# Weight sums formed with the first group's first unit, kept unsplit; more warm-up matmuls; the first gate blocks in another order

## The chip, the cores and the metric

The kernel runs on one core of one Trainium2 chip, as one program. The metric is device time in microseconds (us) of that program. Of the kernel before, three timed runs are given. Where a time stands at a place ("near 252 us"), it is counted from the start of the profiled span.

## The reference

The input is 2 x 1024 rows of 1024 numbers, in fp32. The first block of the network is a gated layer with a sparse gate; the second is a gated feed-forward layer with tiled weights and low-rank terms. Each ends in a residual sum and a layer norm. The change touches only the first half of the first block:

```python
s = silu(einsum('bsh,ih->bsi', x, w_gate))        # 2048 x 2752
_, idx = top_k(-abs(s), k)                        # k = 2752 // 2, per row
s = s with the entries at idx set to 0
s = s * einsum('bsh,ih->bsi', x, w_up)
return einsum('bsi,hi->bsh', s, w_down)
```

The largest half of each row of the gate, by magnitude, is kept exactly, so the gate product must be accurate. The kernel therefore splits each fp32 operand into a high and a low part and multiplies high by high, high by low and low by high.

## The kernel before

The 2048 rows are 16 tiles of 128 rows, in four groups of four tiles (`GT`). The first stage, `gate_up`, runs over groups g, within each over four units u of 688 of the 2752 columns, and within each unit first over the gate ("g") and then over the up product ("u"). It takes about 948 of the 1992 us. Then come the down product and the feed-forward layer, which the change doesn't edit.

A unit's weights are four blocks, B11, B12, B21 and B22: the first digit is the half of the contraction, the second the half of the unit's columns. Each is 128 x 1376 fp32, 688 KB. The up product takes the four blocks one by one, two products each. A product is here 24 matmuls into one pair of PSUM banks, 3.8 us. The gate of most units is done with seven products in place of eight, in Strassen's manner (`GATE`, L42), from blocks and from four weight sums T1 to T4 (`T_AT`, L44: T1 = B12 - B11, T2 = B22 - T1, T3 = B22 - B12, T4 = B21 - T2). Only the first gate of all (g = 0, u = 0) is done with the four plain blocks, in the order of `UP`.

One step is one block or sum. Its work is in three functions:

- `w_load` (L211) issues its DMA from SP, five steps ahead (`LOADS`), into a ring of three raw slots, `wr`.
- `w_prep` (L233), three steps ahead (`AHEAD`), splits it: ACT casts the high part into a ring `wh` (L165), and POOL subtracts it from the raw block into `wl` (L166). For the very first block DVE does the subtraction.
- `products` (L307) issues the matmuls: per product, 16 with the high part of the weights and then 8 with the low part.

`form` (L207) says how a step of the seven-product gate gets its sums. At 2, all four blocks are loaded at once, DVE forms the sums into tiles of the top-k pool (L250), they are split as above, and the split halves are stored to DRAM, two stores of 688 KB for each sum. At 1, in later groups, both halves are read back straight into `wh` and `wl`, with nothing for ACT or POOL to do. The sums are formed in group 0 for the units 1 to 3, and in group 1 for unit 0, which has no seven-product gate in group 0.

The x operands are split the same way, by ACT and DVE (`x_slot`, L191, with sums S1 to S4 formed by DVE at L196 to L201). Those of group 0 are made in the steps of the first unit.

What follows a product: in a plain gate, ACT applies Silu from PSUM (`gate`, L350); in a seven-product gate, `post` combines on DVE and ACT; in the up product, DVE multiplies by the gate result into `mt` (`up`, L358, the row L362). This reading frees the PSUM pair. There are four pairs; one of them stays with the warm-up tile, so that products rotate over three.

`topk` (L369) finds each row's threshold for the group before: six passes in which ACT (L403) counts three of the row tiles and DVE (L400) one, small DVE operations that narrow the bounds (L406 to L426), then two passes a tile (L430, L431) and a final one (L444). It takes its tiles from the same pool as the sums, tags a0 to a3. A scheduler sets the order of instructions on each engine from their dependences and estimated times, so that DVE's operations of `topk`, of `x_slot` and of the products lie mixed.

Ahead of the first stage, a loop (L110) issues `WARM` fp32 matmuls of 128 x 128, each two instructions, on an identity matrix. Their result isn't used.

Of the kernel before, what the change touches and what calls it, by code (L numbers as in the profile page):

```python
# [7 lines left out]
F = mybir.dt.float32  # L8
# [5 lines left out]
ALU = mybir.AluOpType  # L14
# [4 lines left out]
P = 128  # L19
# [9 lines left out]
CW = KH * BW  # L29
# [4 lines left out]
NPR = GT // 2  # L34
# [5 lines left out]
TKAT = (2, "g", 2)  # L40
CACHED = ("T1", "T2", "T3", "T4")
GATE = (("A11", "B11"), ("S2", "T2"), ("S3", "T3"), ("S1", "T1"), ("A12", "B21"), ("S4", "B22"), ("A22", "T4"))  # L42
UP = ("B11", "B21", "B12", "B22")
T_AT = ([("T1", "B12", "B11")], [("T2", "B22", "T1")], [("T3", "B22", "B12")], [], [], [], [("T4", "B21", "T2")])  # L44
LOV = ()
WARM = 14
TAILC = ((0, 512), (512, 768), (768, 1024))


# [13 lines left out]
class Kern:  # L63
# [7 lines left out]
    def run(self):  # L71
# [3 lines left out]
        with ExitStack() as es:  # L75
# [33 lines left out]
            warm = self.tpb()  # L109
            for i in range(WARM):  # L110
                nc.tensor.matmul(warm[:, i % 4, :], self.ident, self.ident, start=True, stop=True)
# [94 lines left out]

    def form(self, i):  # L207
        g, u, w, k = self.steps[i]
        return 0 if w == "u" or g + u == 0 else 2 if g == int(u == 0) else 1

    def w_load(self, i):  # L211
        nc = self.nc
        g, u, w, k = self.steps[i]
        f = self.form(i)
        b = GATE[k][1] if f else UP[k]
        W = self.A["wg" if w == "g" else "wu"]

        def load(q):
            r = self.wr.get()
            k0, n0 = (int(q[1]) - 1) * KH, int(q[2]) - 1  # L220
            self.lastd = nc.sync.dma_start(r.rearrange("p (a b) -> p a b", a=KH), W[2 * u + n0][:, k0 : k0 + KH, :])
            return r

        if f == 2:
            if k == 0:
                self.wb = {q: load(q) for q in ("B11", "B12", "B22", "B21")}
            self.wraw.append(self.wb)
        elif f and b in CACHED:
            self.wraw.append(None)
        else:  # L230
            self.wraw.append(load(b))

    def w_prep(self, i):  # L233
        nc, V = self.nc, self.nc.vector
        g, u, w, k = self.steps[i]
        f = self.form(i)
        b = GATE[k][1] if f else UP[k]
        raw = self.wraw.pop(0)
        hl = self.wh.get(), self.wl.get()
        self.wq.append(hl)  # L240
        if raw is None:
            for x, d in zip(hl, self.tw_d[u, b]):
                nc.sync.dma_start(x.bitcast(F), d)
            return
        if f == 2:
            if k == 0:
                tt = [self.tk.tile([P, 2, CW], F, tag=t, name="tw") for t in (("a3", "a2") if u == 0 else ("a0", "a1"))]
                self.tt = {f"T{j + 1}": tt[j // 2][:, j % 2] for j in range(4)}
            for o, x, y in T_AT[k]:
                V.tensor_tensor(self.tt[o], raw[x], raw.get(y, self.tt.get(y)), ALU.subtract)  # L250
            raw = raw.get(b, self.tt.get(b))
        self.split(*hl, raw, V if i == 0 else nc.gpsimd)
        if f == 2 and b in CACHED:
            for x, d in zip(hl, self.tw_d[u, b]):
                nc.sync.dma_start(d, x.bitcast(F))

    def gate_up(self):
        nc, V = self.nc, self.nc.vector
        ng = self.nt // GT
        self.steps = [(g, u, w, k) for g in range(ng) for u in range(NU) for w in "gu" for k in range(7 if w == "g" and g + u else 4)]  # L260
        self.xfull, self.tkg, self.xs, self.xraw, self.wraw, self.wq, self.li, self.wi = {}, None, {}, {}, [], [], 0, 0
        cc = {}
        xg = self.x_raw(0)
        next(xg)
        for i, (g, u, w, k) in enumerate(self.steps):
            while self.li < min(i + LOADS + 1, len(self.steps)):
                self.w_load(self.li)
                if self.li == 0:
                    list(xg)
                self.li += 1  # L270
            while self.wi < min(i + AHEAD + 1, len(self.steps)):
                j = self.steps[self.wi]
                if j[:2] == (0, 0):
                    for op in {("g", 0): ("A11", "A21"), ("g", 1): ("A12", "A22"), ("u", 1): ("S2",), ("u", 2): ("S1", "S3"), ("u", 3): ("S4",)}.get(j[2:], ()):
                        self.x_slot(op)
                self.w_prep(self.wi)
                self.wi += 1
            wh, wl = (x.rearrange("p (a b) -> p a b", a=KH) for x in self.wq.pop(0))
            if self.form(i):
                a = GATE[k][0]  # L280
                ps = self.pair()[:, :, :BW]
                self.products([(ps[:, p], self.xs[p, a]) for p in range(NPR)], wh, wl, True, True)
                self.post((g, u), k, ps, cc)
            else:
                h = k % 2
                if h == 0:
                    ps = [self.pair()[:, :, :BW] for j in range(2)]
                for j in range(2):
                    self.products([(ps[j][:, p], self.xs[p, f"A{j + 1}{h + 1}"]) for p in range(NPR)], wh, wl, h == 0, h == 1)
                if h:  # L290
                    (self.up if w == "u" else self.gate)((g, u), k // 2, ps, cc)
            if (u, w) == (NU - 1, "u") and g + 1 < ng:
                for op in (("S2", "S1", "S3", "S4"), (), ("A11", "A21"), ("A12", "A22"))[k]:
                    if op == "S2":
                        list(self.x_raw(g + 1))
                    with self.behind():
                        self.x_slot(op)
            if g and (u, w, k) == TKAT:
                self.tkg = self.topk(g - 1)
            if self.tkg:  # L300
                next(self.tkg, None)
            if (g, u, w, k) == (ng - 1, NU - 1, "u", 1):
                self.et = [self.tk.tile([P, NI], d, tag=f"a{j}", name=n) for j, (n, d) in enumerate((("em", F), ("eh", R), ("el", R)))]
                self.d0 = self.down(0, early=3)
                next(self.d0)
# [42 lines left out]
            )  # L348

    def gate(self, un, b, ps, cc):  # L350
        if b == 0:
            cc[un] = [self.ev.tile([P, NPR, 2, BW], F, tag=f"cc{t}", bufs=2, name=f"cc{t}") for t in range(2)]
        for t in range(2):
            self.nc.scalar.activation(cc[un][t][:, :, b], ps[t], AF.Silu)
            if b:
                self.put(self.sp_d, un, t, cc[un][t])

    def up(self, un, b, ps, cc):  # L358
# [585 lines left out]
```

## Time and profile before

| | us |
|---|---|
| median of 3 timed runs | 1996.35 |
| lowest and highest of them | 1995.55, 1996.76 |
| profiled execution, its own time | 1994.28 |
| its span in the profile | 1992.5 |

The busy time of the engines in each stage, and the DMA share there:

| stretch, us | PE | DVE | ACT | POOL | DMA share |
|---|---|---|---|---|---|
| group 0, 0 to 237 | 232.4 | 94.7 | 90.3 | 137.4 | 0.68 |
| group 1, 237 to 474 | 227.6 | 144.7 | 120.4 | 108.6 | 0.76 |
| group 2, 474 to 711 | 233.8 | 137.6 | 117.0 | 93.2 | 0.77 |
| group 3, 711 to 948 | 235.2 | 125.4 | 117.3 | 98.4 | 0.73 |
| down, 948 to 1500 | 519.0 | 336.0 | 234.2 | 354.1 | 0.56 |
| feed-forward, 1500 to 1992.5 | 452.9 | 378.6 | 287.2 | 230.6 | 0.62 |

The stretches are cut by hand where the stages change; neighbours overlap a little at a cut. PE is TensorE's matmuls; DVE, ACT and POOL are VectorE, ScalarE and GpSimd; SP is the engine whose queue issues the DMAs. A row of a timeline gives start, duration, engine, line, operation, output and inputs, shape, count and, in brackets, how long the engine stood idle before it and what it then waited for. The clock is the one that the throttle granted to TensorE, as a share of full speed.

### The profile page before, as it was taken

How to read it: one execution, taken by the hardware profiler on the slowest of the kernel's cores; microseconds unless marked ns; L12 is line 12 of the kernel's file. 1: busy time of each engine (PE TensorE's matmuls, PEld its weight loads, DVE VectorE, ACT ScalarE, POOL GpSimd, SP SyncE). 2: the span in 40 equal slices, each digit the busy share in tenths (PEclk: the TensorE clock that was granted, in tenths of full speed). 3: DMA queues.
4: the chain of work that ended last, by engine and by line, in shares of the span. 5: the costliest groups of instructions: out<-in, count | busy, mean ns of one | idle time of the engine just before them, and what ended most of it. 6: DMA issues, size and time to landing. Idle time of an engine off the chain costs nothing. (4 is left out here: it accounts for less than half of the span.)

```text
span 1992.5 us, 29245 instructions
## 1 busy us (share of the span) xinstructions
PE 1900.8 (95%) x10757; PEld 1762.0 (88%) x10757; DVE 1216.9 (61%) x1791; ACT 966.5 (49%) x1538; POOL 1022.3 (51%) x634
## 2 busy tenths in 40 slices
PE   9999999999999999999898899999998889999998
PEld 8999999999999999999777777777778779898897
DVE  5232646935477345852378935445587988879565
ACT  5323467315852358423575224334334756757363
POOL 5655463434344333344567666665684744626162
PEclk9999999999999999999999999999999999999999
DMA  6677696688757887676844555656556678575661
GB/s 236 240 255 262 216 338 217 237 332 300 271 204 243 338 296 246 249 260 249 293 141 124 182 185 170 208 170 186 169 161 220 227 266 315 176 275 178 221 214 64
DMA packets 156556, 455.14 MB, mean 228 GB/s; under 512 B 23700, under 2 KB 44308, under 8 KB 156408
## 3 DMA queue, kind: packets, MB, share of 16 engines
q1 hardware_dynamic: 156264, 452.97, 65.6%
q8 instruction: 85, 1.39, 0.3%
q14 instruction: 63, 0.52, 0.1%
q10 hardware_dynamic: 144, 0.26, 0.0%
HBM read 346.56 MB, written 106.56 MB: 227 GB/s over the span
## 5 line engine op out<-in xcount | busy, mean ns | idle before, releaser
L166 POOL TENSOR_TENSOR wl<-wr,wh 128x1376 fp32r<-128x1376 f32 (+2 forms) x205 | 598.1, 2925 | 464.3 <-ACT wh L165 441.2
L312 PE MATMUL mm<-wh,xh 128*128 128x344 f32 x1928 | 613.3, 322 | 16.7 <-ACT wh L165 7.1
L312 PE MATMUL mm<-wh,xl 128*128 128x344 f32 x1928 | 611.5, 321 | 0.0
L165 ACT CAST wh<-wr 128x1376 fp32r<-128x1376 f32 (+2 forms) x210 | 246.5, 1182 | 327.5 <-PE mm L312 194.4
L312 PEld LDWEIGHTS mm<-wh,xh 128*128 128x128 f32 x1928 | 364.8, 189 | 19.6 <-ACT wh L165 7.6
L312 PEld LDWEIGHTS mm<-wh,xl 128*128 128x128 f32 x1928 | 364.4, 189 | 0.0
L312 PE MATMUL mm<-wl,xh 128*128 128x344 f32 x1928 | 345.2, 321 | 0.0
L312 PEld LDWEIGHTS mm<-wl,xh 128*128 128x128 f32 x1928 | 313.1, 188 | 0.0
L642 PE MATMUL mm<-wl,mh 128*128 128x512 f32 x680 | 217.4, 400 | 14.5 <-POOL wl L166 14.5
L642 PE MATMUL mm<-wh,mh 128*128 128x512 f32 x680 | 219.4, 405 | 9.0 <-DVE acc L645 6.2
L403 ACT ACTIVATE jk<-a,cur 128x2752 int8<-128x2752 f32 x72 | 186.3, 2588 | 57.3 <-DVE cur L426 42.7
L642 PE MATMUL mm<-wh,ml 128*128 128x512 f32 x648 | 206.3, 398 | 0.0
L601 POOL TENSOR_TENSOR m<-m,ub 128x512 f32<-128x512 f32 (+2 forms) x93 | 108.4, 1165 | 156.8 <-DMA m<-m_d 100.2
L846 POOL TENSOR_TENSOR hf<-hf,gt 128x344 f32<-128x344 f32 x96 | 138.5, 1453 | 80.9 <-DVE gt L840 75.7
L833 PE MATMUL mm<-wh,fh 128*128 128x344 f32 x512 | 168.7, 330 | 11.7 <-DVE gt L840 8.0
L642 PEld LDWEIGHTS mm<-wl,mh 128*128 128x128 f32 x680 | 128.2, 191 | 46.0 <-POOL wl L166 18.6
L835 PE MATMUL mm<-wh,fl 128*128 128x344 f32 x512 | 165.8, 324 | 0.0
L834 PE MATMUL mm<-wl,fh 128*128 128x344 f32 x512 | 165.7, 324 | 0.0
L642 PEld LDWEIGHTS mm<-wh,mh 128*128 128x128 f32 x680 | 124.9, 191 | 34.9 <-issue 6.6
L645 DVE TENSOR_TENSOR acc<-acc,mm 128x1024 f32<-128x1024 f32 x96 | 116.4, 1213 | 52.2 <-PE mm L642 52.0
L600 ACT CAST ub<-u 128x512 bf16<-128x512 uint8 (+2 forms) x93 | 53.1, 571 | 193.4 <-POOL m L601 177.8
L642 PEld LDWEIGHTS mm<-wh,ml 128*128 128x128 f32 x648 | 122.6, 190 | 27.0
(185 smaller groups left out, 2856.6 us busy)
## 6 DMA issues: line engine op xcount, KB each, us to landing
wr<-wu SPq DMA_DIRECT2D x64, 688.0 KB
wr<-wd SPq DMA_DIRECT2D x84, 512.0 KB
wr<-wg SPq DMA_DIRECT2D x53, 688.0 KB
s_d<-cc SPq DMA_DIRECT2D x64, 344.0 KB
m_d<-mt SPq DMA_DIRECT2D x64, 344.0 KB
a<-s_d SPq DMA_DIRECT2D x64, 344.0 KB
wh<-wc_w SPq DMA_DIRECT2D x48, 344.0 KB
wl<-wc_w SPq DMA_DIRECT2D x48, 344.0 KB
```

Source lines behind the costliest of these rows:

```text
L165: self.nc.scalar.copy(hi, raw)
L166: (eng or self.nc.gpsimd).tensor_tensor(lo, raw, hi.bitcast(F), ALU.subtract)
L312: self.nc.tensor.matmul(o, l, r, start=start and n < m and n % (2 * KH) == 0, stop=stop and n >= m and (n - m) % KH == KH - 1)
L403: nc.scalar.activation(jk.bitcast(I8), av[j], AF.Sign, bias=t, scale=-1.0, accum_out=s)
L600: nc.scalar.copy(ub[:, :w], u[:, :w])
L601: nc.gpsimd.tensor_tensor(m[:, :w], m[:, :w], ub[:, :w], ALU.mult)
L642: nc.tensor.matmul(ps[:, h], a, b[:, h * 512 : (h + 1) * 512], start=i == 0, stop=i == len(ops) - 1)
L645: nc.vector.tensor_tensor(out, out, ps.rearrange("p a b -> p (a b)"), ALU.add)
L833: nc.tensor.matmul(o, fh[:, c, :], wh[:, c, :], start=c == 0, stop=False)
L834: nc.tensor.matmul(o, fh[:, c, :], wl[:, c, :], start=False, stop=False)
L835: nc.tensor.matmul(o, fl[:, c, :], wh[:, c, :], start=False, stop=False)
L846: G.tensor_tensor(hf[:, hs], hf[:, hs], gt, ALU.add)
```

## The change

It has three parts, all in the first stage.

- **Sums.** `form` gives 2 only in group 0. For unit 0, DVE forms the four sums while the plain gate of group 0 is prepared: T1 in its second step, T2 and T3 in its third, T4 in its fourth, in tiles a0 and a1. They are stored unsplit, four DMAs of 688 KB, at the preparation of the up product's last step. In the groups 1 to 3, unit 0 loads each sum through the raw ring and splits it on ACT and POOL like a block. The other units keep their stored halves; all sums now use the tiles a0 and a1.
- **Order.** The first gate takes its blocks in the order B11, B12, B22, B21 (`G0`), so that both pairs of column halves are open at once: the first two steps start them, the last two complete them, the second column half first. `gate` allocates its result with the second half and stores it with the first.
- **Warm-up.** `WARM` goes from 14 to 48, that is from 28 to 96 instructions.

```diff
+G0 = ("B11", "B12", "B22", "B21")
 UP = ("B11", "B21", "B12", "B22")
-WARM = 14
+WARM = 48
...
-        return 0 if w == "u" or g + u == 0 else 2 if g == int(u == 0) else 1
+        return 0 if w == "u" or g + u == 0 else 2 if g == 0 else 1
...
-        b = GATE[k][1] if f else UP[k]
+        b = GATE[k][1] if f else (G0 if w == "g" else UP)[k]
...
             if k == 0:
-                self.wb = {q: load(q) for q in ("B11", "B12", "B22", "B21")}
+                self.wb = {q: load(q) for q in G0}
             self.wraw.append(self.wb)
+        elif f and u == 0 and b in CACHED:
+            r = self.wr.get()
+            self.lastd = nc.sync.dma_start(r, self.tw_d[u, b][0])
+            self.wraw.append(r)
         elif f and b in CACHED:
...
+        if g + u == 0 and w == "g":
+            self.b0[b] = raw
         if f == 2:
             if k == 0:
-                tt = [self.tk.tile([P, 2, CW], F, tag=t, name="tw") for t in (("a3", "a2") if u == 0 else ("a0", "a1"))]
+                tt = [self.tk.tile([P, 2, CW], F, tag=t, name="tw") for t in ("a0", "a1")]
...
         self.split(*hl, raw, V if i == 0 else nc.gpsimd)
+        if g + u == 0 and w == "g" and k:
+            if k == 1:
+                tt = [self.tk.tile([P, 2, CW], F, tag=t, name="tw") for t in ("a0", "a1")]
+                self.tt = {f"T{j + 1}": tt[j // 2][:, j % 2] for j in range(4)}
+            for o, x, y in ((), T_AT[0], T_AT[1] + T_AT[2], T_AT[6])[k]:
+                V.tensor_tensor(self.tt[o], self.b0[x], self.b0.get(y, self.tt.get(y)), ALU.subtract)
+        if (g, u, w, k) == (0, 0, "u", 3):
+            for o in CACHED:
+                nc.sync.dma_start(self.tw_d[0, o][0], self.tt[o])
...
-                h = k % 2
-                if h == 0:
+                first = w == "g"
+                h = int((G0 if first else UP)[k][1]) - 1
+                n = int((G0 if first else UP)[k][2]) - 1
+                st, sp = (k < 2, k > 1) if first else (h == 0, h == 1)
+                if st:
                     ps = [self.pair()[:, :, :BW] for j in range(2)]
+                    pss[n] = ps
+                ps = pss[n]
                 for j in range(2):
-                    self.products([(ps[j][:, p], self.xs[p, f"A{j + 1}{h + 1}"]) for p in range(NPR)], wh, wl, h == 0, h == 1)
-                if h:
-                    (self.up if w == "u" else self.gate)((g, u), k // 2, ps, cc)
+                    self.products([(ps[j][:, p], self.xs[p, f"A{j + 1}{h + 1}"]) for p in range(NPR)], wh, wl, st, sp)
+                if sp:
+                    (self.up if w == "u" else self.gate)((g, u), n, ps, cc)
...
     def gate(self, un, b, ps, cc):
-        if b == 0:
+        if b:
             cc[un] = [self.ev.tile([P, NPR, 2, BW], F, tag=f"cc{t}", bufs=2, name=f"cc{t}") for t in range(2)]
         for t in range(2):
             self.nc.scalar.activation(cc[un][t][:, :, b], ps[t], AF.Silu)
-            if b:
+            if b == 0:
                 self.put(self.sp_d, un, t, cc[un][t])
```

In the built program, TensorE's order of the first gate is both products of B11, then one each of B12, B22 and B21 for one half of the rows (the first tile of each pair), then those of B12, B22 and B21 for the other half. B12's second product waits until ACT's first Silu has read a PSUM pair.

More of the change, by code (lines that the diff above doesn't have):

```diff
@@ L236, in w_prep @@
         f = self.form(i)
-        b = GATE[k][1] if f else UP[k]
+        b = GATE[k][1] if f else (G0 if w == "g" else UP)[k]
         raw = self.wraw.pop(0)
@@ L261, in gate_up @@
         self.xfull, self.tkg, self.xs, self.xraw, self.wraw, self.wq, self.li, self.wi = {}, None, {}, {}, [], [], 0, 0
-        cc = {}
+        cc, self.b0 = {}, {}
+        pss = {}
         xg = self.x_raw(0)
```

## The prediction

> **What bounds the kernel now.** I read the page's first part, then the waits in front of TensorE, then the stretches where the change acts, engine by engine.
>
> ```profile
> PE 1900.8 (95%) x10757; PEld 1762.0 (88%) x10757; DVE 1216.9 (61%) x1791; ACT 966.5 (49%) x1538; POOL 1022.3 (51%) x634
> ```
>
> TensorE is busy 95% of 1992.5 us and every other engine about half. So an edit is worth what it does to TensorE's gaps, plus the slow matmuls that follow a gap. The change touches three places in the gate and up stage. The first is the start (PE, timeline):
>
> ```profile
> 1.43 6.24 PE L111 MATMUL mm<-ident 128*128 128x128 f32 x28 [1.43 <-POOL ident masks.py:199]
> 10.55 0.42 PE L312 MATMUL mm<-wh,xh 128*128 128x344 f32 x1 [2.88 <-ACT wh L165]
> ...
> 31.62 0.42 PE L312 MATMUL mm<-wh,xh 128*128 128x344 f32 x1 [0.33 <-ACT cc L354]
> ```
>
> [...]28 warm-up instructions run to 7.67, TensorE idles 2.88, the first product starts at 10.55. The granted clock, by microsecond (PEclk is the third figure from the right):
>
> ```profile
> 10.00:11.00 1.00, 0.45 (x2) 0.46 (x3) 0.47 (x1) 1.00 (x3) 0.00 (x0) 0.92 1.10 440
> 11.00:12.00 1.00, 1.00 (x5) 1.00 (x5) 1.00 (x1) 1.00 (x4) 0.00 (x0) 0.50 1.02 422
> ```
>
> It is 0.50 until about 14.2: 13 matmuls take 0.284 us each, not the stage's 0.158, a loss of 13 x 0.126 = 1.6 us.
>
> The second place is the first unit's gate of the second group, where the weight sums are formed (timelines of DVE, ACT and PE):
>
> ```profile
> 247.66 1.59 DVE L250 TENSOR_TENSOR tw<-wr 128x1376 f32<-128x1376 f32 x1
> ...
> 249.34 1.34 ACT L165 CAST wh<-tw 128x1376 fp32r<-128x1376 f32 x1 [0.42 <-DVE tw L250]
> ...
> 252.30 0.42 PE L312 MATMUL mm<-wh,xh 128*128 128x344 f32 x1 [4.20 <-ACT wh L165]
> ```
>
> The sum T1 waits on DVE behind four operand splits, the cast of its successor behind that, and TensorE idles 4.20 us. Then the clock is 0.57 over 253 to 257: some 12 matmuls at +0.126, 1.5 us. Together **5.7 us**.
>
> The third is a top-k step of the third group (DVE and PE):
>
> ```profile
> 582.60 0.17 DVE L406 TENSOR_SCALAR up<-cur 128x4 int32<-128x4 f32 x1 [5.37 <-ACT jk L403]
> ...
> 586.16 3.09 DVE L434 TENSOR_TENSOR df<-iota,hi 128x32 f32<-128x32 f32 x1
> 589.19 0.86 DVE L362 TENSOR_TENSOR mt<-mm,cc 128x688 f32<-128x688 f32 x1
> ...
> 590.11 0.43 PE L312 MATMUL mm<-wh,xh 128*128 128x344 f32 x1 [3.22 <-DVE mt L362]
> ```
>
> The product mt, which frees a PSUM pair, stands on DVE behind L406, which waits for ACT's count, and behind two passes of 3.09 us. TensorE loses 3.22 and, at clock 0.83 over 590 to 600, about 1.5: **4.7 us**.
>
> **The change, part by part.**
>
> *Sums taken out of the second group.* DVE's four sums, the eight stores of halves and the four simultaneous B loads leave the gate at 248. In their place T1 to T4 are four raw 688 KB loads in the ordinary ring, five steps ahead, then one ACT cast (1.34 us) and one POOL subtraction (3.15) each. Seven subtractions are 22 us of a 26.6 us gate (7 x 3.8), so POOL holds the pace; ACT has its casts done two steps ahead. The 5.7 us go: next late is the first up block's cast, wanted 3 to 4 us after it is ready. **-5.7 us.**
>
> *Third and fourth group.* For the first unit, eight reads of halves become four reads of sums (-2.8 MB per group; in all, 8 stores and 16 reads of 688 KB become 4 and 12), while ACT gains 2 x 4 x 1.34 = 10.7 us and POOL 2 x 4 x 3.15 = 25.2 us. Both are half idle, and the top-k passes that burden DVE begin two units later. If POOL's cover failed, each late subtraction would cost at most its 3.15 us. I take 0, keeping -1 (the reads delay TensorE by nothing longer than 1.1 us there) to +3.
>
> *Top-k tiles.* The sums now always use tiles a0 and a1, so the first group's top-k gets its tiles earlier and DVE's order around 590 changes: in the built program this mt stands ahead of L406 and not behind it. Its product is complete near 579, ten microseconds before it ran. **-4.7 us.** Next late are DVE's count passes, which no matmul waits for. The order shifts in other units and in the down stage by one or two instructions too; the stalls there (5.65 and 6.21 us near 1080 and 1142) stay behind the same four passes of 3 us. I take 0, with ±3.
>
> *Warm-up.* 68 more instructions. At the row's pace (6.24 / 28, start to start 0.214) all 96 end at 1.43 + 20.5 = 21.9. [...] It matters little, as the next part hides it: nothing on DVE, ACT or POOL in the first unit waits for TensorE before the first Silu.
>
> *Sums in the first unit.* The blocks come as B11, B12, B22, B21, and DVE gets four sums of two SBUF inputs, 1.59 us each, among its operand splits. SP issues B21's load only when T1 has read its operand and freed a slot. In numbers: DVE follows the old rows to 22.8, T1 runs to 24.35, the load is issued at 24.4 and lands some 3.5 to 4 us later (that long took the pair at 18.18), the cast is done at 29.4. Then POOL must subtract for B21. DVE meanwhile has a dense run: xl and xt operations of 0.6, T2, T3 and T4 end at 36.1. How POOL fares beside a dense DVE has two rows:
>
> ```profile
> 14.94 3.21 POOL L166 TENSOR_TENSOR wl<-wr,wh 128x1376 fp32r<-128x1376 f32 x1 [13.36 <-ACT wh L165]
> ...
> 25.45 7.05 POOL L166 TENSOR_TENSOR wl<-wr,wh 128x1376 fp32r<-128x1376 f32 x1 [3.73 <-ACT wh L165]
> ```
>
> The first got in at once (and DVE's next operation then took 3.66 instead of 0.68). The second waited 3.9 us through seven DVE operations, until DVE itself had to wait for a cast at 29.5. [...] The case at 29.4 is that row's: POOL comes out of idleness to a DVE that runs back to back. I take the row: the subtraction runs 36.1 to 39.2.
>
> TensorE's fifth product needs that half after 112 matmuls. Before, it read its low half at 29.86. So it is 39.2 - 29.86 = 9.3 us late, has idled over 6 us, and pays the cold spell of the two other stalls, 1.5: **+10.8 us**, with the warm-up hidden inside. (Even at the slow pace of 0.214 TensorE would get there at 39.6.) If POOL got in at 29.4, DVE would slip by 3.1 and with it the last casts ahead of ACT's table load (1.28) and first Silu, which would end at 37.0; the sixth product, at 31.62 before, would be 5.4 late: +5.4 to +6.9. Queued on SP behind the waiting B21 load are the stores of T1 and T2, the second group's first x loads and the first up blocks; TensorE wants the first of these only three products of 3.8 us after the stall, near 52, over 6 us after it can be split. The four stores of 688 KB fall where the DMA share is 0.5 to 0.7.
>
> **Sum**: -5.7 - 4.7 + 10.8 = +0.4 us. On the profiled execution's 1994.28 that is 1994.7; that run lies 2.1 below the median of the timed ones, 1996.35, so the forecast against the median is **1996.7**.
>
> **Rivals.** About 0.2%, 4.0 us, is what can be told from no change.
>
> 1. *POOL gets its turn.* For it: the row of 14.94. Against: DVE has no gap in reach at 29.4. Sum -5.7 - 4.7 + 5.4 = -5.0: **1991.4**.
> 2. *Slower: the top-k stall stays.* Place: the up steps of the third group. If ACT's counts come later than today, because casts were added in front of them, mt again stands behind an L406 that waits; it decides once the count ends more than about 3 us after the pair's product. Then only the 5.7 is earned: -5.7 + 10.8 = +5.1: **2001.4**. Against: the built order.
> 3. *Both*: POOL in turn, stall kept: -0.3, **1996.1**, no change.
>
> **How the numbers follow.** Forecast 0.38, first rival 0.22, second 0.25, third 0.10, others 0.05 (mostly slower: a new POOL or DVE collision). With ±3 for the shifted order, forecast spills a fifth of its chance beyond the bound, slightly more upward: faster 0.15 + 0.07 = 0.22, slower 0.17 + 0.10 + 0.05 = 0.32, within 0.46. Range: from the first rival less 1.5 to the second plus 2: 1990 to 2003.5.
>
> **What will show it.** In the changed kernel: warm-up ending near 14.9 (or 21.9) and no clock of 0.50 at 11 to 14; B21's POOL subtraction long (about 9 us, mostly waiting) and TensorE idle some 6 us near 33 to 39, or short and the wait ended by Silu; no gap over 1 us near 252; none before mt near 590. I am wrong if the fifth product starts before 34, if the sums' raw loads reach the ring late in groups two to four, or if new gaps of 2 us stand in the down stage.

## The result, and the profile after

The changed kernel takes 2012.8 us (2006.56 to 2015.07, 6 runs) against 1995.95 for the kernel before on the same chip: ratio 1.0068, interval 1.0053 to 1.0084. It is slower; the forecast was 1996.7 and no change. The profiled execution takes 2009.09 us, span 2007.3: 14.8 us more than the span before.

The page's first part again, for the changed kernel:

```profile
PE 1912.3 (95%) x10825; PEld 1773.2 (88%) x10825; DVE 1261.1 (63%) x1791; ACT 974.7 (49%) x1546; POOL 1047.1 (52%) x642
```

POOL has 8 instructions more and 25 us more, as the forecast counted; DVE has as many instructions as before and 44 us more. The same number of instructions takes longer, so something holds them up. The waits of TensorE in the first stage, from its timeline (columns as before; in the changed code L334 are the matmuls, L384 is the product in `up`, L166 the casts and L167 the subtractions of the splits, L409 and L425 the top-k's passes on ACT):

```profile
27.80 2.00 PE L334 MATMUL mm<-wl,xh 128*128 128x344 f32 x8 [3.76 <-POOL wl L167]
256.64 0.43 PE L334 MATMUL mm<-wh,xh 128*128 128x344 f32 x1 [2.02 <-DVE mt L384]
285.30 0.65 PE L334 MATMUL mm<-wh,xh 128*128 128x344 f32 x1 [3.26 <-ACT wh L166]
497.93 0.65 PE L334 MATMUL mm<-wh,xh 128*128 128x344 f32 x1 [3.98 <-DVE mt L384]
621.68 0.42 PE L334 MATMUL mm<-wh,xh 128*128 128x344 f32 x1 [2.31 <-DVE mt L384]
736.80 0.43 PE L334 MATMUL mm<-wh,xh 128*128 128x344 f32 x1 [3.38 <-DVE mt L384]
763.55 0.66 PE L334 MATMUL mm<-wh,xh 128*128 128x344 f32 x1 [3.26 <-ACT wh L166]
```

Waits alone do not make the sum, as a wait can bring slow matmuls behind it (behind the wait of 2.02 they start 0.287 us apart from 257.4 to 260.6, at clock 0.50, and not 0.157). So the 241 products of the first stage were numbered in both traces and the differences of their starts taken. A row below is how much the difference grows across a stretch:

| stretch | grows by, us | forecast |
|---|---|---|
| first unit of group 1 | +6.5 | +10.8 |
| first unit of group 2 (248 before) | +5.0 | -5.7 |
| the rest of group 2 | -5.9 | 0 |
| first unit of group 3 | +6.8 | 0 |
| second unit of group 3 (590 before) | -5.0 | -4.7 |
| third unit of group 3 | +5.0 | 0 |
| first unit of group 4 | +10.2 | 0 |
| other parts of groups 1, 3 and 4 | -0.1 | 0 |
| after the first stage | -7.7 | 0 |
| sum | +14.8 | +0.4 |

The loss is in the first units: +28.5 us in four places.

**The first unit of group 1.** POOL's and DVE's timelines:

```profile
14.89 12.85 POOL L167 TENSOR_TENSOR wl<-wr,wh 128x1376 fp32r<-128x1376 f32 x1 [13.30 <-ACT wh L166]
...
24.12 0.68 DVE L202 TENSOR_TENSOR xt<-xr,xt 128x512 f32<-128x512 f32 x1
24.82 3.47 DVE L167 TENSOR_TENSOR xl<-xr,xh 128x512 fp32r<-128x512 f32 x1
```

POOL asks at 14.89 for the low half of B12, which needs 3.15 us and has it at 27.74. Until 24.8 DVE runs one operation behind the other, without a gap. Then it waits 0.02 us for a cast, POOL gets in, and DVE's next operation takes 3.47 instead of 0.68. In the kernel before, POOL asked at 14.94 and got in at once, beside a DVE just as dense; why it was let in there isn't shown. Below, *exclusion* means what these rows show: the subtractions of POOL and of DVE do not run side by side, and one waits until the other has ended.

**The start of the gate in the later groups**, here group 3 (ACT, POOL, then DVE):

```profile
485.96 2.51 ACT L409 ACTIVATE a<-a 128x2752 f32<-128x2752 f32 x1 [6.53 <-DMA a<-s_d]
488.37 0.18 ACT L409 ACTIVATION_READ_ACCUMULATOR a<-a 128x1 f32 x1
488.45 1.33 ACT L166 CAST wh<-wr 128x1376 fp32r<-128x1376 f32 x1
...
489.86 3.18 POOL L167 TENSOR_TENSOR wl<-wr,wh 128x1376 fp32r<-128x1376 f32 x1 [11.48 <-ACT wh L166]
493.19 6.88 POOL L167 TENSOR_TENSOR wl<-wr,wh 128x1376 fp32r<-128x1376 f32 x2 [0.15 <-ACT wh L166]
...
490.33 6.75 DVE L167 TENSOR_TENSOR xl<-xr,xh 128x512 fp32r<-128x512 f32 x2 [9.42 <-ACT xh L166]
497.01 1.64 DVE L384 TENSOR_TENSOR mt<-mm,cc 128x688 f32<-128x688 f32 x2
```

The first of these POOL operations splits T3, the two of the next row split T1 and then B21 (T2's, at 475.22, meets no operand split). In the kernel before nothing stands there for the sums. DVE's two operand splits, 1.3 us together, take 6.75: the first waits for T3's subtraction to end, the second for T1's. The mt that frees a PSUM pair stands behind them, and TensorE, idle from 493.95, gets its pair at 497.93. (The two mt, with one operand in PSUM, take 0.86 each beside B21's subtraction and are not held.) T3's cast comes as late as 488.45 because ACT, in order, first waited 6.53 us for the load of a top-k pass (8.08 and 5.90 in groups 2 and 4); no run moved that pass.

**The first up product**, here of group 2 (ACT):

```profile
271.57 1.34 ACT L166 CAST wh<-wr 128x1376 fp32r<-128x1376 f32 x1 [8.00 <-DMA wr<-tw0T4h]
273.35 2.51 ACT L409 ACTIVATE a<-a 128x2752 f32<-128x2752 f32 x1 [0.44 <-DMA a<-s_d]
...
276.28 2.59 ACT L425 ACTIVATE jk<-a,cur 128x2752 int8<-128x2752 f32 x1 [0.34 <-DVE cur L416]
...
281.35 2.58 ACT L425 ACTIVATE jk<-a,cur 128x2752 int8<-128x2752 f32 x1
...
283.93 3.80 ACT L166 CAST wh<-wr 128x1376 fp32r<-128x1376 f32 x3
```

ACT, in order, waits 8.00 us for the raw T4, then does four passes of the top-k (273.35 to 283.9), and only then the cast for the first up block, which TensorE wants at 282.0.

### The profile page after: what moved, and what is told of

Its sections match the earlier page's. It is cut to its first block, busy times and chain, and to the rows that moved or that the text cites. A ratio compares the mean times of both kernels' runs of the same rounds, so it can differ in the third digit from the quotient of the medians.

```text
span 2007.3 us, 29376 instructions
## 1 busy us (share of the span) xinstructions
PE 1912.3 (95%) x10825; PEld 1773.2 (88%) x10825; DVE 1261.1 (63%) x1791; ACT 974.7 (49%) x1546; POOL 1047.1 (52%) x642
## 5 line engine op out<-in xcount | busy, mean ns | idle before, releaser
L167 POOL TENSOR_TENSOR wl<-wr,wh 128x1376 fp32r<-128x1376 f32 (+2 forms) x217 | 636.4, 2942 | 475.2 <-ACT wh L166 449.1
L334 PE MATMUL mm<-wh,xh 128*128 128x344 f32 x1928 | 618.3, 324 | 21.1 <-DVE mt L384 12.4
L334 PE MATMUL mm<-wh,xl 128*128 128x344 f32 x1928 | 616.0, 323 | 0.0
L166 ACT CAST wh<-wr 128x1376 fp32r<-128x1376 f32 (+2 forms) x222 | 261.9, 1191 | 347.3 <-PE mm L334 149.8
L334 PEld LDWEIGHTS mm<-wh,xh 128*128 128x128 f32 x1928 | 368.9, 191 | 24.7 <-DVE mt L384 13.9
L334 PEld LDWEIGHTS mm<-wh,xl 128*128 128x128 f32 x1928 | 368.4, 191 | 0.0
L334 PE MATMUL mm<-wl,xh 128*128 128x344 f32 x1928 | 345.7, 321 | 3.8 <-POOL wl L167 3.8
L334 PEld LDWEIGHTS mm<-wl,xh 128*128 128x128 f32 x1928 | 313.4, 188 | 4.0 <-POOL wl L167 4.0
L425 ACT ACTIVATE jk<-a,cur 128x2752 int8<-128x2752 f32 x72 | 186.3, 2587 | 54.4 <-DVE cur L448 37.0
L866 ACT ACTIVATE pa<-pa 128x344 f32<-128x344 f32 x256 | 123.1, 483 | 49.5 <-DVE pa L864 47.9
```

Source lines behind the costliest of these rows:

```text
L166: self.nc.scalar.copy(hi, raw)
L167: (eng or self.nc.gpsimd).tensor_tensor(lo, raw, hi.bitcast(F), ALU.subtract)
L334: self.nc.tensor.matmul(o, l, r, start=start and n < m and n % (2 * KH) == 0, stop=stop and n >= m and (n - m) % KH == KH - 1)
L425: nc.scalar.activation(jk.bitcast(I8), av[j], AF.Sign, bias=t, scale=-1.0, accum_out=s)
L866: nc.scalar.activation(pa[:, r], pa[:, r], AF.Copy, scale=0.5, accum_out=part[:, r, b : b + 1])
```

## The experiments

The kernel before ran on the same chip each time; the ratio is to it. The chips differ by up to 3 us, so two runs from different chips are compared by their distance from the kernel before.

| run | median, us | before, us | ratio, interval |
|---|---|---|---|
| the change | 2012.80 | 1995.95 | 1.0068, 1.0053 to 1.0084 |
| e1 | 2015.12 | 1999.21 | 1.0076, 1.0048 to 1.0104 |
| e2 | 2002.15 | 1999.21 | 1.0027, 1.0013 to 1.0042 |
| e3 | 2006.74 | 1999.21 | 1.0044, 1.0030 to 1.0058 |
| e4 | 1987.73 | 1999.21 | 0.9948, 0.9934 to 0.9962 |
| e5 | 1989.94 | 1996.76 | 0.9970, 0.9957 to 0.9983 |
| e6 | 1990.20 | 1996.76 | 0.9958, 0.9944 to 0.9973 |
| e7 | 1996.26 | 1996.76 | 1.0001, 0.9991 to 1.0012 |
| e8 | 2010.12 | 1996.76 | 1.0064, 1.0049 to 1.0079 |
| e9 | 2001.73 | 1996.67 | 1.0023, 1.0013 to 1.0034 |
| e10 | 1979.13 | 1996.67 | 0.9906, 0.9883 to 0.9929 |
| e11 | 1991.85 | 1996.67 | 0.9974, 0.9961 to 0.9987 |
| e12 | 1980.85 | 1996.12 | 0.9917, 0.9891 to 0.9944 |

One thing limits how they may be read. The scheduler orders all engines anew for each program. The traces, compared by line, operation and tiles, show how much. In e1, e3, e4, e6, e9, e10 and e12 the order is that of the changed kernel, but for the instructions that the edit moves between POOL and DVE and up to some fifteen others on an engine. e2 has the order of the kernel before through the first stage, and e7 that of e6; behind it 62 and 125 of DVE's 1141 instructions stand elsewhere. e8 is reordered in the first stage too (on DVE 46 of 650). e5 differs from the changed kernel in group 2, most of all on ACT, and has the order of the kernel before behind the first stage; e11 has e5's order. At these places a time is that of the edit and of a new order.

**e4: T2 and T3 split by DVE in groups 2 to 4.**

```diff
-        self.split(*hl, raw, V if i == 0 else nc.gpsimd)
+        self.split(*hl, raw, V if i == 0 or (g and u == 0 and b in ("T2", "T3")) else nc.gpsimd)
```

> The changed kernel with the low halves of T2 and T3 in the first unit of groups 2 to 4 made by VectorE instead of GpSimd. Exclusion theory: the operand splits of 6.75 us at 490 fall to 1.3, mt is no longer late and the three waits at the second product of those gates (2.0, 4.0, 3.4 us, each with about 2.3 us of cold matmuls behind it) go: 10 to 16 us gained, about 1999. Ring and queue theory (ScalarE waits in order for the sums' loads through a ring of three): those waits stay, or return at the first up product, and under 5 us are gained.

It gains more than expected: 28 us against the changed kernel, each counted from the kernel before on its chip (25 by the bare medians), 21.8 of them in the first stage by products, and it is faster than the kernel before. The same place in its trace (DVE, then POOL):

```profile
480.57 1.59 DVE L167 TENSOR_TENSOR wl<-wr,wh 128x1376 fp32r<-128x1376 f32 x1 [7.04 <-ACT wh L166]
482.08 1.29 DVE L167 TENSOR_TENSOR xl<-xr,xh 128x512 fp32r<-128x512 f32 x2
483.29 1.65 DVE L384 TENSOR_TENSOR mt<-mm,cc 128x688 f32<-128x688 f32 x2
...
483.94 3.17 POOL L167 TENSOR_TENSOR wl<-wr,wh 128x1376 fp32r<-128x1376 f32 x1 [16.60 <-ACT wh L166]
```

The first row is T3's subtraction, the last T1's. DVE has more to do and is done earlier: the two xl take 1.29, mt starts 2.7 us after the first of these operations, and POOL starts after them. ACT's cast is no earlier for it: it ends 3.0 us before the gate's first product does, in the changed kernel 4.2. The waits at the second product are gone in all three groups. DVE's order is otherwise the same. The waits at the first up product shrink too, but there one cast has also moved ahead of a top-k count on ACT, so e4 alone cannot say which of the two did it.

**e9, the control: T1 and T4 instead.** POOL gives up as much.

```diff
-b in ("T2", "T3")
+b in ("T1", "T4")
```

> The control: as the run with T2 and T3 on VectorE, but with T1 and T4 instead. GpSimd is relieved of as much, at another place: its subtractions for T2 and T3 still stand beside the operand splits at the start of the gate. Exclusion theory: the waits for mt at the second product of the three gates stay, about 6 us each with their cold matmuls. In the built order ScalarE's cast for the first up block now stands ahead of a top-k count, so the waits at the first up products (3.3 us at 285 and 763) should go: 8 to 12 us gained, 2001 to 2005. If it was GpSimd's load as such, the waits at the second product go too and it reaches about 1988.

2001.73, inside the span that the exclusion theory gave, but the waits did not stay as they were. At the same place (DVE, then PE):

```profile
489.50 3.85 DVE L167 TENSOR_TENSOR xl<-xr,xh 128x512 fp32r<-128x512 f32 x2 [9.70 <-ACT xh L166]
493.27 1.64 DVE L384 TENSOR_TENSOR mt<-mm,cc 128x688 f32<-128x688 f32 x2
...
494.19 0.43 PE L334 MATMUL mm<-wh,xh 128*128 128x344 f32 x1 [1.46 <-DVE mt L384]
```

The expectation had T2 and T3 beside the operand splits; by the order of the casts it is T3 and T1, so this edit takes away one of the two neighbours. T3's subtraction still holds the first xl; the second now escapes, so the wait is 1.46 instead of 3.98 (2.10 for 3.38 in group 4; in group 2, where only the split behind T3's stands ahead of mt, 1.20 for 2.02). With T3 on DVE, in e4, it was gone. The waits at the first up products, 3.26 twice, are gone, with ACT's cast ahead of a top-k count in the built order. e4 and e9 relieve POOL equally and leave different waits, so it is not POOL's load that counts at the start of the gate, but which operation stands beside which; and the loss at the gate's end goes where the cast does not queue behind the top-k. New waits of 1.1 to 2.2 us for mt and cc appear in later units. Why T4's load comes so late, whether from the ring of three raw slots or from the transfers ahead of it, was not tried.

**e10: all four sums split by DVE.**

```diff
-b in ("T2", "T3")
+b in CACHED
```

> All four sums' low halves on VectorE in groups 2 to 4. If the rest of the waits in those gates (0.5 to 2 us in the run with T2 and T3) still comes from GpSimd's pace, 2 to 5 us below that run, about 1984. If VectorE's added 6.4 us per gate now delays the results that free PSUM, it is slower than that run by 2 to 6 us.

The fastest of all: 1979.13, ratio 0.9906, and more than the 2 to 5 us expected below e4: 6 counted from the kernel before, 8 in the first stage by products. Behind the warm-up only three waits of 0.8 us or more are left to TensorE until the down stage begins (PE):

```profile
28.20 2.64 PE L334 MATMUL mm<-wl,xh 128*128 128x344 f32 x8 [4.31 <-POOL wl L167]
891.04 0.40 PE L334 MATMUL mm<-wh,xh 128*128 128x344 f32 x1 [2.03 <-DMA wh<-tw3T1h]
940.80 0.69 PE L664 MATMUL mm<-wh,eh 128*128 128x512 f32 x2 [1.17 <-DVE mt L384]
```

**e5, e11: halves kept, as before, from group 2 on.**

```diff
-        elif f and u == 0 and b in CACHED:
+        elif f and g == 1 and u == 0 and b in CACHED:
...
-        if f == 2 and b in CACHED:
+        if (f == 2 or f and g == 1 and u == 0) and b in CACHED:
```

> The changed kernel, but the sums of the first unit are kept split from the second group on: group 2 stores the halves it has made, groups 3 and 4 read them back, with nothing there for ScalarE or GpSimd. That prices 'kept unsplit'. By the product ledger the first unit's gates of groups 3 and 4 lose 6.9 and 10.2 us in the changed kernel; if the split on GpSimd is the cause, both go: some 15 to 17 us gained, about 1998. If the loss comes from the top-k's new place beside those gates, it stays.

1989.94, some 23 us under the changed kernel and below the 1998 expected. The first units of groups 3 and 4 give back all they had lost. The surplus is in the first unit of group 2 (9.2 us), where the waits at the second product and at the first up product shrink as well, and in the third unit of group 3, where 5.0 go. In group 2 the order differs; in group 3 it is the same, but POOL's work comes at another moment. Neither is shown to be the halves' doing. **e11** adds `(g and u == 0 and b in ("T2", "T3"))` on DVE to it.

> The run with stored halves, and T2 and T3 of group 2 split by VectorE. In that run's trace the second product of group 2's gate no longer waits, so exclusion has nothing left to cost there: within 2 us of it, about 1989 to 1991. If GpSimd still delays something in group 2, 3 to 5 us faster.

1991.85: by the medians no change. The trace is less clear: its first stage is 4.0 us shorter than that of e5, as the other branch has it, and the rest, in the same order, 7.9 us longer. So this run doesn't tell whether POOL still delays something in group 2.

**e3: the first gate's low halves by DVE.**

```diff
-        self.split(*hl, raw, V if i == 0 else nc.gpsimd)
+        self.split(*hl, raw, V if g + u == 0 and w == "g" else nc.gpsimd)
```

> The changed kernel with the low halves of all four blocks of the first gate made by VectorE, so that GpSimd asks for nothing there. If mutual exclusion of GpSimd and VectorE is what delays the first unit, the wait of 3.76 us at 27.8 and its cold matmuls go, and the first unit ends 1.5 to 4 us later than before instead of 6.5: 3 to 5 us gained. If VectorE's load as such is the bound (four sums and three halves of 1.59 us, 11.1 us more than before), the wait only changes its name and the unit ends as late or later.

The wait at 27.8 goes, and 5.7 us of the first unit with it, so that its up part starts 0.8 us later than before the change, though DVE has 11 us more work in it than it had there. Exclusion, not DVE's load.

**e6, e12: both cures.** e6 is e3 with e4, e12 is e3 with e10.

> The changed kernel with both cures: the first gate's low halves, and those of T2 and T3 in groups 2 to 4, by VectorE. Exclusion theory: the gains of the two single runs add, -5.7 in the first unit and -22 in the later gates: about 1982, under the kernel before by 14 to 18. If both act on one shared delay, it stays near 1987.7.

> The run with all four sums' low halves on VectorE, and the first gate's low halves on VectorE too. The only long wait left in the first stage of that run is the 4.3 us at 28 for GpSimd's low half, with some 1.5 us of cold matmuls. In the changed kernel the same edit took 5.7 us out of the first unit. If it adds: about 1974. When it was added to the run with T2 and T3, 3.9 us came out of the first unit but a new wait in group 3's gate took 3.7 back; if the order of the later work is again what decides, it ends within 2 us of 1979.

Neither adds. In e6 the first unit is 3.9 us earlier than in e4; then, in groups 3 and 4, TensorE waits 3.54 and 2.16 us for a combining step on DVE (`cc`, L353) where it did not in e4 (there 1.96 in group 2). In e12 the first unit's up part starts 4.6 us earlier than in e10, and waits of 0.9 to 2.2 us in later units take it back. The rest of the program is the same in order. Why a unit that is early by some microseconds meets the top-k less well is open.

**e1, e2, e7: the warm-up.** e1 is the changed kernel, e7 is e6, each with `WARM = 14`; e2 is the kernel before with `WARM = 48`.

> The changed kernel with 14 warm-up matmuls again. If the longer warm-up costs what it pushes back, the first unit is some 3 us earlier and the time about 2010. If the first unit's delay comes from GpSimd shut out by VectorE, the warm-up is hidden behind it: the first products start near 10.5 at clock 0.50 again, the product that waits for its low half still waits until about 27.8, and the time stays within 2 us of the changed kernel's 2012.8.

> The kernel before with 48 warm-up matmuls and nothing else. Here nothing hides it: in the changed kernel's trace the warm-up ended near 13.7 and the first product started at 13.73 against 10.55, with no cold matmuls behind it, so +3.2 - 1.6 = +1.6 us (1998). If the pace of the warm-up did not double, +9.8 us.

> The same with 14 warm-up matmuls. With nothing left that hides the warm-up, the shorter one starts the first product near 10 instead of 13.7 but runs 13 matmuls cold: 0.5 to 2 us faster than with 48. If the shorter warm-up moves GpSimd and VectorE against each other as in the kernel with 14 above, it does not matter here, as GpSimd asks for nothing in the first gate.

In e2 the first unit's up part starts 1.1 us later than in the kernel before, as the expectation's sum has it (1.6) and not the 9.8 of the row's pace (21.9 - 10.55 - 1.6), and its first stage ends 0.9 later; its median is 0.27% higher. In e1 the products begin 4.0 us earlier and the unit ends 4.2 us later than in the changed kernel (PE):

```profile
9.71 0.43 PE L334 MATMUL mm<-wh,xh 128*128 128x344 f32 x1 [3.22 <-ACT wh L166]
...
31.73 0.66 PE L334 MATMUL mm<-wl,xh 128*128 128x344 f32 x1 [11.65 <-POOL wl L167]
```

POOL, which asked at 14.98, got in even later here: in the same order of instructions DVE had no gap before 28.74, POOL's operation ended at 31.67, and TensorE waited 11.65 us. Counted from the kernel before, e1 is as slow as the changed kernel (15.9 and 16.9 us). So the long warm-up costs nothing there, since the first unit waits for POOL anyway. In e7 the first unit is 0.7 us earlier than in e6, as expected, but the whole is slower: TensorE waits 2.9 to 4.1 us for `cc` (L353) near 269, 505 and 741, in e6's order of instructions. Behind the first stage the order is another.

**e8: the kernel before with the tiles a0 and a1.**

```diff
-for t in (("a3", "a2") if u == 0 else ("a0", "a1"))]
+for t in ("a0", "a1")]
```

> The kernel before with the sums of the first unit in the top-k tiles a0 and a1 instead of a3 and a2, the rest unchanged. It tells what the tiles' choice alone does to the top-k's place. If it moves the wait near 590 and brings the 6 to 8 us that the changed kernel gains in the rest of group 2 and in the down stage, the time is 5 to 12 us below the kernel before. If those gains come from the lighter DMA (no stores of halves in group 2), it stays within 3 us.

Neither: it is 13 us slower. The sums, formed in group 2, now hold tiles that the top-k wants, and the reordered group 2 gets waits of 3.25, 4.99 and 4.07 us near 342, 425 and 450. The wait near 590 stays (3.20 at 603). So the choice of tiles alone brings neither the gains of the changed kernel in group 2 nor the one near 590. The lighter DMA does not explain the former either: e5 and e11, with group 2's stores back, gain 3.9 and 6.6 us in the rest of group 2, where the changed kernel gains 5.9. Both gains came with the moved sums; by what, stays open.

## Why the prediction was wrong

**Busy shares stood in for a timetable.** The step that failed is "Third and fourth group: ... Both are half idle ... I take 0, keeping -1 to +3". It measured +6.8 and +10.2. POOL had the time, but its operations for T3 and T1 at the start of the gate stand beside the operand splits, and the prediction had itself described what they do to each other, in the first unit only. e4 and e9 show that this is the cause at the gate's start; e5, without the splits, has nothing left of the loss in these two units. The range missed it because +3 was the length of one late subtraction, not the wait of everything that queues behind DVE (3.98 and 3.38 us at the second product), plus cold matmuls.

**"The 5.7 us go: next late is the first up block's cast, wanted 3 to 4 us after it is ready."** The old wait went, but the group's first unit grew by 5.0: 2.02 came at the second product, again by exclusion, and 3.26 at just that cast, which was 3 us late and not 3 early. "ACT has its casts done two steps ahead" overlooked that ACT waits in order, 8.00 us for T4's load here and 8.08 for the load of a top-k pass ahead of T3's cast.

**The first unit.** The mechanism was right (a POOL starved by a dense DVE, with the warm-up hidden inside), and so was the choice of the row of 25.45. The size was off: +6.5 for +10.8. POOL starved already at B12, asked for at 14.89, where the forecast had kept the old rows up to 22.8; DVE, not blocked there, was earlier with all that followed. No run shows the 14.9 that the prediction names for the end of the warm-up, nor the row's 21.9: it ended near 13.7, as its instructions start 0.21 us apart up to 4.6 and 0.11 from there on.

**Top-k at 590.** -5.0 for -4.7: the number and the new place of mt were right. The reason given, the tiles a0 and a1, is not shown, as e8 has them and keeps the wait. "Next late are DVE's count passes, which no matmul waits for" was wrong; 25 us later the wait is back (POOL, then DVE):

```profile
614.80 3.16 POOL L167 TENSOR_TENSOR wl<-wr,wh 128x1376 fp32r<-128x1376 f32 x1 [13.82 <-ACT wh L166]
...
615.19 5.66 DVE L452 SCALAR_TENSOR_TENSOR ku<-a,hi 128x2752 f32<-128x2752 f32 x1
620.77 0.86 DVE L384 TENSOR_TENSOR mt<-mm,cc 128x688 f32<-128x688 f32 x1
```

A pass of 3.1 us takes 5.66 ahead of an mt that TensorE waits for: +5.0 in that unit. The rows suggest exclusion once more: POOL's subtraction ends at 617.96, and the pass 2.9 us later, about its own length. In e4, in the same order, POOL's subtraction starts at 602.85, after this pass has begun at 602.05, and the pass takes 3.08. No run tried this alone. The second rival had this outcome, at another place.

**After the first stage** the changed kernel gains 7.7 us, where the forecast had 0 with ±3 and said of the wait near 1080 that it would stay. It did not (PE, before and after):

```profile
1080.45 1.11 PE L622 MATMUL tp<-ident,m 128*128 128x128 f32 x4 [5.65 <-DVE ml L627]
...
1101.09 0.66 PE L644 MATMUL tp<-ident,m 128*128 128x128 f32 x4 [2.11 <-DVE ml L649]
```

The new order goes with this gain. All eight programs that have the changed kernel's order there wait at most 2.1 us at that place, and all but one take 1039.4 to 1044.0 us from the start of the first stage's last product to the end; the kernel before and the two programs with its order there, e5 and e11, wait 5.6 to 5.7 and take 1049.5, 1049.9 and 1057.8. The exception is e9, with 1051.2 in the slowest of its 22 executions. What in the order does it was not tried. So this gain, like the one of 5.9 in group 2, hid a part of the loss, and neither was forecast.

The rivals had no case in which the new POOL work meets DVE in the later groups; it was left to "others", at 0.05.

## What to carry to other kernels

Before moving work onto an engine that is half idle, look up what stands beside it at that moment on the engine whose operations exclude its own, and who queues behind that one: two subtractions of 3.2 us on an idle GpSimd each held a VectorE operation (two took 6.75 us and not 1.3), and with them a PSUM release and TensorE (3.98 us). With the subtractions of all four sums on VectorE, the busier of the two, the kernel was faster than either version (e10). And price an edit by where its instructions land in each engine's order, not by its share of busy time.

## What was not expected of the hardware

- How long GpSimd can be kept out: 9.7 us in the changed kernel (asked at 14.89, run in the last 3.15 of 12.85), 13.6 in e1 (16.70 less 3.15), by operations of 0.7 to 1.6 us, none of which is long.
- The price of a wait in cold matmuls does not follow its length. The changed kernel by stretches of 3.41 us (first the length, then PE's busy time; PEclk is the third figure from the right), around the waits of 2.02 and of 3.38 us:

```profile
253.91:257.32 3.41, 1.39 (x9) 1.10 (x8) 3.41 (x3) 3.41 (x5) 3.26 (x2) 1.00 0.00 0
257.32:260.73 3.41, 3.41 (x14) 3.41 (x13) 3.41 (x3) 0.92 (x2) 3.41 (x2) 0.50 0.99 328
...
731.78:735.19 3.41, 1.64 (x11) 1.35 (x9) 3.41 (x2) 2.46 (x4) 3.25 (x2) 1.00 0.00 0
735.19:738.60 3.41, 1.79 (x11) 1.80 (x12) 3.41 (x4) 0.74 (x1) 3.41 (x2) 1.00 0.30 113
738.60:742.01 3.41, 3.41 (x24) 3.41 (x23) 3.41 (x5) 0.00 (x0) 0.36 (x1) 1.00 1.02 271
```

The slow spells of a trace begin whole multiples of 3.41 us apart, here at 28.63, 257.32, 284.63, 496.25, 622.55 and 762.49, and the stretches above are cut on that grid. The wait of 2.02 lies in one stretch, and the next runs at 0.50; the longer wait is divided by a border into 1.77 and 1.62, and the clock stays at 1.00. In all 14 traces, from 20 to 940 us, each full-speed stretch of the grid with 1.91 us or more of idle TensorE is followed by one at 0.50 (36 cases), and none with 1.80 or less.
